# Loading the first experts' weights one round earlier on SyncE's queue, with two small edits beside it

## The chip, the cores and the metric

One Trainium2 chip, one of its cores. The metric is the time of one execution on the device, in microseconds. The kernel is one launch; nothing is computed on the host.

## The reference, cut to what matters

The inputs are x (32 sequences of 56 tokens, 256 wide, so 1792 tokens), a context of 32 x 1500 rows of 256, a mask, and the weights of four layers. Each layer normalizes x and adds its result to x:

```python
x = x + _L0_xattn_ref(_layernorm(x), ctx, ...)   # decayed running sum over 1500 context rows, two projections, mean, layernorm
x = x + _L0_ffn_ref(_layernorm(x), ...)          # 16 experts of 176, each token takes its best 6
x = x + _L1_xattn_ref(_layernorm(x), ctx, mask)  # attention over the masked context
x = x + _L1_ffn_ref(_layernorm(x), ...)          # 2 experts of 1024, each token takes 1
```

The layer that matters here is the second one:

```python
scores = softmax(h @ gate_w.T); topk_w, topk_idx = top_k(scores, 6)
for e in range(16):
    g = h @ w_gate[e].T; u = h @ w_up[e].T
    y = y + cw[:, e:e+1] * (silu(g) * u @ w_down[e].T)
```

## The kernel before, in words

**First stage, lines 228 to 904.** The context is read once, one sequence of 1.5 MB at a time, by SyncE's DMA queue (`load_ctx`, L155) into a ring of five slots. TensorE sums each sequence with the decay weights (`count_in`, L339); after it has used slot b it lets the load of sequence b + 5 begin. Two sequences share one tile of 128 rows, a pair; there are 16 pairs, 0 to 15. A loop of 15 rounds runs over a list written out by hand (`steps`, then `ends`, L751 to 765): each round handles several pairs at different depths. Round p counts the context of later pairs, projects and normalizes pair p, and for pair p - 1 writes the normalized rows: `second_norm` (ScalarE, L563) makes them in a tile of the pool `xn`, which has four buffers, so that the tile of pair p is that of pair p - 4; `away` (L569) stores it to the scratch tensor `xn0` in HBM over SyncE's queue. I call these norm p and store p. The same rows go on to the router: transposed (`turned`), gated (`gate`), the six best experts marked (`best`), ranked within their expert (`ranks`, `counted`, `places`), and sorted into blocks of 128 rows of one expert by products with one-hot matrices (`ones_at` on VectorE, `more_ones` on GpSimd, L674, `last_ones` on ScalarE, L692; `tokens_in`, ScalarE, L655, multiplies in the token numbers; `sorted_in`, TensorE, L702). Only two one-hot tiles exist, so those of pair p are written after the products of pair p - 1.

**After the loop** the last three pairs a, b, c = 13, 14, 15 are finished by a straight list of calls (L775 to 903), which ends with the table `idx` of the rows of each block (VectorE, L902) and the weights `wgt` (ScalarE, L903). `busy(n)` (L683) puts n products of 128 x 512 into TensorE's queue whose result nobody reads.

**The weights of the 16 experts** live in one tile, `w0_sb`. `load_w0_up` (L206) issues four transfers of 1408 KB for the gate and up halves, in rows of 704 bytes. `w0_down_pieces` (L222) yields 26 small transfers of 16 to 176 KB for the down half; `some_pieces(n)` issues the next n of them. All of this, like the context and the stores, is issued by SyncE in program order. In the built program every transfer of that queue uses one of eight completion counters in turn, and is issued only when the transfer eight places before it has landed.

**Second stage, L905 to 1230.** The experts run over 95 blocks. Block i needs its rows gathered from `xn0` by GpSimd's indirect DMA (L1092, the first eight together), transposed by TensorE (L191) and copied by ScalarE (L193), and then the gate and up products (L933), the transposes (L951) and the down products (L960). The weight of a block is addressed by a register, so the first gate-up product waits for every transfer into `w0_sb`, and the first gather for every store into `xn0`.

Of the kernel before, what the change touches and what calls it, by code (L numbers as in the profile page):

```python
# [22 lines left out]
NP = B // 2  # L23
# [37 lines left out]
def xattn_ffn_kernel(  # L61
# [141 lines left out]
    def load_w0_up():  # L203
        for m, w in ((0, wg0), (1, wu0)):
            for k in range(KD):
                nc.sync.dma_start(  # L206
                    out=w0_sb[:, :, (2 * k + m) * F0 : (2 * k + m + 1) * F0],
                    in_=w[:, k, :].rearrange("p (e f) -> p e f", f=F0),
                )

    def w0_down_pieces():

        half = E0 // 2
        for e in range(half):
            for c in range(2):
                r = 0
                while r < H0:
                    f = e * F0 + c * H0 + r
                    n = min(H0 - r, P - f % P)
                    o = 2 * KD * F0 + c * D  # L220
                    k = f // P
                    yield lambda r=r, n=n, e=e, o=o, f=f, k=k: nc.sync.dma_start(  # L222
                        out=w0_sb[r : r + n, e :: half, o : o + D],
                        in_=wd0[f % P : f % P + n, k :: half * F0 // P, :][:, 0:2, :],
                    )
                    r += n

    with tc.tile_pool(name="p1", bufs=1) as p1, tc.tile_pool(name="p3", bufs=3) as p3, tc.tile_pool(
# [185 lines left out]
        def first_stats(o):  # L414
            for p in range(o, o + 4):
                V.bn_stats(out=st[:, p, :], in_=xr[:, p, :])
                V.bn_aggr(out=mva[:, p, :], in_=st[:, p, :])
            inverse_root(rsa[:, o : o + 4], mva[:, o : o + 4, 1])

        def first_bias(o):  # L420
            q = slice(o, o + 4)
            V.scalar_tensor_tensor(nba[:, q], mva[:, q, 0], -1.0, rsa[:, q], ALU.mult, ALU.mult)
# [145 lines left out]
        def away(p):  # L568
            nc.sync.dma_start(out=xn0[p * P : (p + 1) * P, :], in_=pend[p]["xn"])  # L569
# [23 lines left out]
        def scores_out(p):  # L593
            A.copy(lgs[p % 2][:, 0:E0], pend[p]["lp"][:, 0:E0])
# [25 lines left out]
        def ranks(p):  # L620
            rk = ps.tile([P, 512], F32, tag="ps", name="rk")
            PE.matmul(rk[:, 0:E0], lhsT=before, rhs=sel[:, p, :], start=True, stop=False)
            PE.matmul(rk[:, 0:E0], lhsT=ones, rhs=chosen[:, 1 - p % 2], start=False, stop=True)
            keep(p, rk=rk)
# [7 lines left out]
        def places(p):  # L632

            nm, pr = pend[p]["nm"], pend[p]["pr"]
            V.tensor_scalar(lvl[:, p, :], pos[:, p, :], -0.5 - P / 2, ROUND, ALU.add, ALU.add)
            V.tensor_scalar(lvl[:, p, :], lvl[:, p, :], -ROUND, 1.0 / P, ALU.add, ALU.mult)
            off = small.tile([P, E0], F32, tag="off", name="off")
            V.scalar_tensor_tensor(
                off, lvl[:, p, :], -float(P), pos[:, p, :], ALU.mult, ALU.add
            )  # L640
            v = vals[:, p % 2]
            V.tensor_tensor(
                v[:, :, 0, :], e16.unsqueeze(1).to_broadcast([P, E0, NLP]),
                lvl[:, p, :].unsqueeze(2).to_broadcast([P, E0, NLP]), ALU.is_equal,
            )
            V.reciprocal(nm[:, 1:2], nm[:, 1:2])
            V.scalar_tensor_tensor(
                v[:, :, 1, :], v[:, :, 0, :], nm[:, 1:2],
                pr.unsqueeze(2).to_broadcast([P, E0, NLP]), ALU.mult, ALU.mult,
            )  # L650
            keep(p, off=off)

        def tokens_in(p):
            v = vals[:, p % 2]
            A.activation(v[:, :, 0, :], v[:, :, 0, :], AF.Copy, scale=ids[:, p : p + 1])  # L655

        def hots(p, h):
            t = pend[p].setdefault("hots", {})
            if h not in t:
                t[h] = ohp.tile([P, NE, P], F32, tag="oh", name="oh")  # L660
            return t[h]

        def ones_at(p, h, n=NE):

            o = NE * h
            V.tensor_tensor(
                hots(p, h)[:, 0:n], iota.unsqueeze(1).to_broadcast([P, n, P]),
                pend[p]["off"][:, o : o + n].unsqueeze(2).to_broadcast([P, n, P]), ALU.is_equal,
            )
# [9 lines left out]
        def busy(n, w=512):  # L679

            for _ in range(n):
                d = psa.tile([P, 512], F32, tag="acc", name="d")
                PE.matmul(  # L683
                    d[:, 0:w], lhsT=ident, rhs=ones[:, 0:1].to_broadcast([P, w]),
                    start=True, stop=True,
                )

        def last_ones(p, h, n):

            t, off = hots(p, h)[:, n:NE], pend[p]["off"]  # L690
            for i in range(n, NE):
                A.activation(  # L692
                    t[:, i - n], iota, AF.Abs, bias=off[:, NE * h + i : NE * h + i + 1], scale=-1.0
                )
            A.activation(t, t, AF.Relu, bias=ones[:, 0:1], scale=-1.0)
# [19 lines left out]
        def low_ones(p):  # L715
            ones_at(p, 0)
# [16 lines left out]
        pieces = list(w0_down_pieces())  # L733


        def some_pieces(n):
            for _ in range(n):
                if pieces:
                    pieces.pop(0)()
# [22 lines left out]
        for p in range(last):  # L762
            for step, d in steps if p == last - 1 else steps + ends:
                if 0 <= p + d < NP:
                    step(p + d)
            if p < 3:
                first_stats(4 * p + 4)
                first_bias(4 * p + 4)
            if p == NP - 4:
                load_w0_up()  # L770
            if p > NP - 4:
                some_pieces(6)


        at_ = slots[B % NRING].rearrange("p j d -> p (j d)")[0:1, CW - 2 * E0 * NLP :]  # L775
        G.memset(at_, 0.0)
        at_ = at_.rearrange("p (e o l) -> p e o l", e=E0, o=2)
        a, b, c = last - 2, last - 1, last
        scores_out(a)
        sum_in_columns(c)  # L780
# [24 lines left out]
        away(b)  # L805
        second_norm(c)
        away(c)
        some_pieces(len(pieces))
        places(a)
        turned(b)  # L810
        more_high_ones(a)
# [22 lines left out]
        PE.matmul(tot[:, 0:E0], lhsT=ones, rhs=chosen[:, b % 2], start=False, stop=True)  # L834
        more_high_ones(b)
        ranks(c)
        busy(2)
        real = p2.tile([P, NL, E0], F32, name="real")
        V.tensor_tensor(
            real, tot[:, 0:E0].unsqueeze(1).to_broadcast([P, NL, E0]), lev, ALU.is_gt  # L840
# [20 lines left out]
        for k in range(4):  # L861
# [3 lines left out]
                rhs=ones[0:1, 0:1], start=True, stop=True,  # L865
            )
        low_ones(c)
        last_ones(c, 1, 6)
        tokens_in(c)
        ones_at(c, 1, 6)  # L870
        sorted_low(c)
        blk = p2.tile([P, 4], F32, name="blk")
# [963 lines left out]
```

## Time and profile before

| | |
|---|---|
| runs before, us | 703.46 median of 3 (700.73 to 703.96) |
| profiled execution, us | 743.97, its span 742.3 |
| busy share of the span | PE 91%, PEld 59%, DVE 52%, POOL 43%, ACT 35% |
| mean granted TensorE clock | 0.955 |
| SyncE's queue (q1) | 56042 packets, 100.31 MB, 38.6% of 16 engines' span |
| first gather issued, us from the span's start | 180.53 |
| first gate-up product of the experts | 186.37 |

The profiled execution is 40.5 us longer than the median of the runs shown. PE is the matrix engine, PEld its weight loads, DVE VectorE, ACT ScalarE, POOL GpSimd; SPq is SyncE's queue, whose rows are DMA issues. A timeline row is: start in us, length in us, engine, line, operation, output<-input, count, and in brackets how long the engine was idle before it and what ended that. A row of a table by stretches has the busy us of each engine (count of instructions in parentheses), then the granted clock, then the DMA engines' busy share and their GB/s.

### The profile page before, as it was taken

The page shows a single profiled execution, that of the slowest core. Times are in us where ns is not written, and L with a number is a line of the kernel's source. Part 1 is how long each engine was busy: PE and PEld are TensorE (multiplying, and loading weights), DVE is VectorE, ACT ScalarE, POOL GpSimd, SP SyncE. Part 2 cuts the span into 40 slices and gives each one's busy share as a digit, 9 for nine tenths or more (in the row PEclk, how much of TensorE's full clock was granted, in tenths as well). Part 3 has the DMA queues.
Part 4 walks back from the last instruction along what each step waited for, and adds up shares of the span by engine and source line. Part 5 has one row for each costly group of instructions (what it writes and reads, how often), then busy time and mean ns, then how long its engine had stood idle before and what let it go on. Part 6 is the DMA issues. An engine that isn't in the chain of part 4 may idle for free.

```text
span 742.3 us, 13524 instructions
## 1 busy us (share of the span) xinstructions
PE 674.1 (91%) x4111; PEld 434.3 (59%) x4111; DVE 386.9 (52%) x1310; ACT 258.5 (35%) x772; POOL 318.0 (43%) x416
## 2 busy tenths in 40 slices
PE   7789999998799888898898888999897999999997
PEld 3345565654577565566676655566554666666564
DVE  5548888885256344343353436568787332323232
ACT  0224555542244333333343332476552111111110
POOL 3104454544543664667656655558423302122111
PEclk7858999998899999999999999999999999999999
DMA  8999999995489874444444444595941201010100
GB/s 272 337 406 404 410 411 411 384 287 147 133 260 282 292 217 149 121 128 128 135 128 136 128 124 119 149 329 79 333 143 62 88 15 33 32 38 28 35 30 18
DMA packets 71273, 136.63 MB, mean 184 GB/s; under 512 B 8026, under 2 KB 43772, under 8 KB 71196
## 3 DMA queue, kind: packets, MB, share of 16 engines
q1 hardware_dynamic: 56042, 100.31, 38.6%
q0 software_dynamic: 14096, 34.52, 17.1%
q10 hardware_dynamic: 1058, 0.86, 0.4%
q8 instruction: 38, 0.62, 0.4%
q14 instruction: 39, 0.32, 0.1%
HBM read 109.54 MB, written 26.77 MB: 184 GB/s over the span
## 4 chain that ended last, share of the span: by engine, by line
PE 65%; DVE 4%; issue 2%; ACT 2%; SPq 1%; DMA 1%; POOL 0%; another core or an unknown queue 0%; POOLq 0%; ACTq 0%; DVEq 0%
PE gu L933 30%; PE y L960 19%; PE tp L951 4%; PE tp L191 3%; PE tp L1064 3%; PE sp L1294 2%; PE op L1329 2%; SPq L222 1%; ACT xT L193 1%; PE tp L1053 1%; PE tp L1321 1%; PE sp L1288 1%; DMA w_sb<-in_wd 1%; DMA xs<-pay,to 0%; POOL oh L674 0%
## 5 line engine op out<-in xcount | busy, mean ns | idle before, releaser
L933 PE MATMUL gu<-w_sb,xT 128*128 x380 | 134.3, 476 | 29.4 <-ACT xT L193 19.8
L939 ACT ACTIVATE sg<-gu 128x176 f32<-128x176 f32 (+1 forms) x155 | 53.3, 344 | 247.0 <-PE gu L933 213.0
L1092 POOL DMA_INDIRECT xb<-xn,idx x95 | 94.0, 989 | 95.5 <-PE tp L191 43.3
L945 DVE SCALAR_TENSOR_TENSOR hs<-sg,wgt,gu 128x176 f32<-128x176 f32 x95 | 37.7, 397 | 154.5 <-ACT sg L939 129.2
L933 PE MATMUL gu<-ring,xT 128*128 x240 | 113.8, 597 | 0.0
L933 PEld LDWEIGHTS gu<-w_sb,xT 128*128 128x128 f32 x380 | 69.9, 192 | 65.4 <-ACT xT L193 27.8
L960 PE MATMUL y<-w_sb,hT 88*128 x380 | 98.6, 382 | 1.6 <-ACT yb L1100 1.6
L1007 POOL DMA_INDIRECT g<-ys,early x78 | 74.6, 956 | 35.3 <-issue 20.4
L943 DVE TENSOR_TENSOR hs<-sg,gu 128x256 f32<-128x256 f32 x60 | 25.3, 421 | 112.2 <-ACT sg L939 108.3
L951 PEld LDWEIGHTS tp<-ident,hs 128*88 128x88 f32 (+1 forms) x310 | 40.3, 130 | 58.7 <-issue 47.9
L960 PEld LDWEIGHTS y<-w_sb,hT 88*128 88x128 f32 x380 | 65.0, 191 | 7.4 <-ACT yb L1100 2.0
L1580 POOL DMA_INDIRECT out<-ob,ti x15 | 14.8, 990 | 126.9 <-DVE ob L1577 126.6
L674 POOL TENSOR_SCALAR oh<-iota,off 128x128 f32<-128x128 f32 x60 | 42.5, 722 | 59.0 <-PE owned L702 39.8
L953 DVE COPY hT<-tp 88x256 f32<-88x256 f32 (+1 forms) x155 | 64.4, 415 | 4.8 <-PE y L960 4.0
L933 PEld LDWEIGHTS gu<-ring,xT 128*128 128x128 f32 x240 | 45.6, 192 | 33.3 <-issue 30.5
L339 PE MATMUL acc<-ring,cz 128*32 128x256 f32 x768 | 57.0, 438 | 5.8 <-DMA ring<-in_cx 5.4
L960 PE MATMUL y<-ring,hT 128*128 x240 | 61.7, 380 | 0.0
L951 PE MATMUL tp<-ident,hs 128*88 128x128 f32 (+1 forms) x310 | 59.5, 274 | 0.0
L193 ACT COPY xT<-tp 128x256 f32<-128x256 f32 x110 | 41.0, 373 | 41.9 <-PE y L960 21.3
L1100 ACT COPY yb<-y 128x256 f32<-128x256 f32 x95 | 35.7, 376 | 47.0 <-PE y L960 27.2
L191 PE MATMUL tp<-ident,xb 128*128 128x128 f32 x220 | 42.5, 275 | 0.9 <-DMA xb<-xn,idx 0.9
L960 PEld LDWEIGHTS y<-ring,hT 128*128 128x128 f32 x240 | 41.0, 190 | 3.3
(315 smaller groups left out, 967.5 us busy)
## 6 DMA issues: line engine op xcount, KB each, us to landing
ring<-in_cx SPq DMA_DIRECT2D x32, 1536.0 KB
ys<-yb SPq DMA_DIRECT2D x95, 128.0 KB
ring<-in_cx SPq DMA_DIRECT2D x16, 384.0 KB
extra<-in_cx SPq DMA_DIRECT2D x16, 384.0 KB
xs<-zrow SPq DMA_DIRECT2D x5, 771.0 KB
w_sb<-in_wg SPq DMA_DIRECT2D x2, 1408.0 KB
w_sb<-in_wu SPq DMA_DIRECT2D x2, 1408.0 KB
xn<-xn SPq DMA_DIRECT2D x16, 128.0 KB
```

The lines of the kernel that those rows point to most:

```text
L191: PE.transpose(tp[:, k * P : (k + 1) * P], xn[:, k * P : (k + 1) * P], ident)
L193: A.copy(xT.rearrange("p k c -> p (k c)"), tp[:, 0 : KD * P])
L339: PE.matmul(acc[Q * g : Q * g + Q, 0:D], lhsT=cz[:, j, 1 - h : 1 - h + Q], rhs=c[:, j, :], start=(h == 0 and m == 0), stop=(h == 1 and m = ...
L674: G.tensor_scalar(hots(p, h)[:, i, :], iota, pend[p]["off"][:, NE * h + i : NE * h + i + 1], None, ALU.is_equal,)
L933: PE.matmul(gu[:, 0 : 2 * fp], lhsT=xT[i][:, k, :], rhs=w[:, bass.ds(at[i] + (u * piece + k * 2 * fp), 2 * fp)], start=(k == 0), stop=(k = ...
L939: A.activation(sg, gu[:, 0:fp], AF.Silu)
L945: V.scalar_tensor_tensor(hs[i, u], sg, wgt[:, i : i + 1], up, ALU.mult, ALU.mult)
L951: PE.transpose(tp[0:h, c * P : (c + 1) * P], a[:, c * h : (c + 1) * h], ident)
L953: V.tensor_copy(hT[i, u], tp[0:h, 0 : 2 * P])
L960: PE.matmul(y[i][:, 0:D], lhsT=a[:, c * P : (c + 1) * P], rhs=w[0:h, bass.ds(at[i] + (u * piece + doff + c * D), D)], start=(u == 0 and c ...
L1007: G.indirect_dma_start(out=g, out_offset=None, in_=ys0[0 : n * P, :], in_offset=bass.IndirectOffsetOnAxis(ap=at[:, p, k : k + 1], axis=0),)
L1092: G.indirect_dma_start(out=xb, out_offset=None, in_=xn0, in_offset=bass.IndirectOffsetOnAxis(ap=idx[:, i : i + 1], axis=0),)
```

## The change

In the loop, `load_w0_up` is called at the end of round 11 and not 12, and the rounds after it issue eight down pieces each and not six. The pieces that are left after the loop are issued ahead of everything in the list that follows, and not after the stores of pairs 14 and 15. One of two unread products after `ranks(c)` goes. `tokens_in(c)` is called ahead of `last_ones(c, 1, 6)`.

```diff
@@ -766,15 +766,16 @@
-            if p == NP - 4:
+            if p == NP - 5:
                 load_w0_up()
-            if p > NP - 4:
-                some_pieces(6)
+            if p > NP - 5:
+                some_pieces(8)
 
 
         at_ = slots[B % NRING].rearrange("p j d -> p (j d)")[0:1, CW - 2 * E0 * NLP :]
         G.memset(at_, 0.0)
         at_ = at_.rearrange("p (e o l) -> p e o l", e=E0, o=2)
+        some_pieces(len(pieces))
         a, b, c = last - 2, last - 1, last
@@ -805,7 +806,6 @@
         away(b)
         second_norm(c)
         away(c)
-        some_pieces(len(pieces))
         places(a)
@@ -834,7 +834,7 @@
         ranks(c)
-        busy(2)
+        busy(1)
@@ -865,8 +865,8 @@
         low_ones(c)
+        tokens_in(c)
         last_ones(c, 1, 6)
-        tokens_in(c)
         ones_at(c, 1, 6)
```

On SyncE's queue the order from the last context load on was: store 11, four gate/up loads, store 12, 6 pieces, store 13, 6 pieces, stores 14 and 15, 14 pieces. It becomes: four gate/up loads, store 11, 8 pieces, store 12, 8 pieces, store 13, 10 pieces, stores 14 and 15. No other engine's order changes but for the missing product on PE and the place of one instruction on ACT.

## The prediction

> **What bounds the kernel now.** I read the page first: TensorE is busy for 91% of the span, but the change touches only the passage from the router to the experts, so what counts is which wait ends last there. The chain of waits, in that stretch, says:
>
> ```profile
> 181.69 4.13 DMA w_sb<-in_wd
> 185.82 0.55 issue
> 186.37 1.56 PE gu L933 x4
> ```
>
> The last down piece is issued at 181.69, lands at 185.82, and lets the first gate-up product go at 186.37. After that the experts keep TensorE in work to the end, so a shift of this product shifts the end. Second, SyncE's own timeline, the queue whose order changes:
>
> ```profile
> 131.70 0.37 SPq L155 DMA_DIRECT2D ring<-in_cx  x1
> 134.89 0.34 SPq L569 DMA_DIRECT2D xn<-xn  x1
> 135.32 10.62 SPq L206 DMA_DIRECT2D w_sb<-in_wg  x2
> 146.00 9.35 SPq L206 DMA_DIRECT2D w_sb<-in_wu  x2
> 155.44 3.66 SPq L569 DMA_DIRECT2D xn<-xn  x1
> 159.14 4.88 SPq L222 DMA_DIRECT2D w_sb<-in_wd  x6
> 164.44 0.37 SPq L569 DMA_DIRECT2D xn<-xn  x1
> 165.06 4.82 SPq L222 DMA_DIRECT2D w_sb<-in_wd  x6
> 169.98 1.77 SPq L569 DMA_DIRECT2D xn<-xn  x2
> 171.80 10.74 SPq L222 DMA_DIRECT2D w_sb<-in_wd  x14
> ```
>
> From 135.32 on this queue hardly rests: the weights are as late as they are because it is never free. Two regimes must be told apart, by the table of stretches (its last three columns are granted clock, DMA share, GB/s):
>
> ```profile
> 134.00:136.00 2.00, 2.00 (x30) 0.92 (x26) 1.90 (x10) 1.14 (x4) 0.00 (x0) 1.00 1.03 410
> ...
> 158.00:160.00 2.00, 2.00 (x6) 0.93 (x5) 1.39 (x5) 0.50 (x2) 0.00 (x0) 1.00 1.15 334
> ...
> 168.00:170.00 2.00, 2.00 (x3) 0.96 (x4) 2.00 (x3) 0.67 (x4) 2.00 (x2) 0.50 0.45 106
> ```
>
> To about 162 the DMA engines are full (share above 1): the long issues of L206 are a full queue pushing back. After that they are half idle and the issue itself is the pace, 0.8 us for each piece.
>
> Last, who else arrives at the experts, and the two places at which the change will be felt:
>
> ```profile
> 160.99 1.08 ACT L563 ACTIVATE xn<-xr,mv 128x256 f32<-128x256 f32 x2
> ...
> 179.31 0.26 DVE L902 CAST idx<-bl 128x95 int32<-128x95 f32 x1 [1.48 <-PE bl L898]
> ...
> 180.53 1.19 POOL L1092 DMA_INDIRECT xb<-xn,idx  x1 [9.82 <-ACT wgt L903]
> ```
>
> The gathered rows are transposed, and ScalarE's copy of block 0 (L193) runs from 184.57 for 0.37: ready at 184.94, only 1.4 us before the product. So two chains end nearly together: weights (186.37) and rows (about 185.0).
>
> **Edit 1a, the four loads ahead of store 11.** Program order lets SyncE issue them after the context load at 131.70, at 132.1 and not 135.32: 3.2 us earlier. The Trainium skill's DMA: Bandwidth & Descriptors (Rules for kernel authors) advises to issue a transfer early and wait late. By that rule all that follows on the queue moves up 3.2 us. By the row it cannot: at 134 to 136 the engines move 410 GB/s of context already queued ahead, and the loads drain behind it whenever they are issued. All they gain is that store 11 no longer stands ahead: 128 KB / 410 GB/s = 0.3 us. I take the row. SyncE is then free for the first piece at 159.14 - 0.3 = 158.8.
>
> **Edit 1b, store 11 behind the loads.** It now takes the place that store 12 had, issued by 159. Store 12 landed just before 165.06: the piece issued then waited for it (SyncE's waits list 0.2 us at L222 for the store), since a transfer waits for the one eight places before it. So store 11 lands at 165.0 - 0.3 = 164.7. Norm 15 writes the buffer of norm 11, so it may not start before; the row of L563 shows it starting at 161.5. ScalarE stalls for 3.2 us, and behind it stand both row copies for the router (L581), so the gates of pairs 14 and 15, and everything down to `idx`.
>
> **Edit 1c, the last two stores behind all pieces.** 26 pieces cost 4.88 + 4.82 + 10.74 = 20.4 us. Between them now stand stores 12 and 13, about 0.45 each, and some 0.3 us of waits for counters: 158.8 + 20.4 + 0.9 + 0.3 = 180.4. So the last piece is issued 2.1 us sooner (182.54 before), and weights would land near 183. But stores 14 and 15 begin only then. Before, they began at 169.98, and the trace's semaphore record has GpSimd's wait for the last one end at 173.13, 3.15 us on: now 180.4 + 3.15 = 183.6. The first gather waits for them. Before, it started at 180.53, 0.96 after `idx` (179.57), and 4.5 us later block 0 could have begun (185.03). Now: 183.6 + 0.96 + 4.5 = 189.1, against 186.37. That is +2.7.
>
> **Edits 2 and 3.** The unread products:
>
> ```profile
> 167.81 3.76 PE L683 MATMUL d<-ones,ident 128*128 128x512 f32 x4
> 171.50 1.94 PE L702 MATMUL owned<-oh,vals 128*32 128x128 f32 x32
> ```
>
> Two products took 3.76 us at half clock; without one, the sort of pair 14 starts 1.9 sooner, though its upper half waits for GpSimd's one-hots to 170.7, so 1.7 are left. With the token numbers ahead of the two compares, the last sort (L702 at 175.27) no longer waits 0.63 for them. Downstream VectorE gains only the 0.4 it waited for the products, and the products for `idx` come after its last compare: 1.0 us in sum. Set against the stall: `idx` at 179.57 + 3.2 - 1.0 = 181.8, the gather could go at 182.7. The stores hold it until 184.6, so these edits are worth nothing while that cover stands, and 1.0 if it is gone. The skill's TensorE: Matmul & The Clock Gate (HAM oscillation) warns of idle gaps over 3.4 us; by it the missing product could cost the clock. In the row of 168 to 170 the clock is at 0.50 with both products there, so at this place nothing is left to lose. Bounds: 0 to -1.0.
>
> **The clock at the first blocks.** TensorE idles from 183 to 186 before block 0, and the chain shows block 0's gate-up at 1.56 and block 1's, from 188.82, at 2.48: the clock falls between. Now it idles till 189 (the unread products that fill the time end about 3.3 after `wgt`, near 185.4), so I expect block 0 to fall in the half clock as well: +0.9. Bounds: 0 (the drop moves with the work) and +2 (a third block too).
>
> **Sum:** 2.7 + 0.9 = 3.6 us, on 743.97 of the profiled execution 747.6. The 40.5 us between that and the median lie in places the page doesn't name; I carry the shift over unscaled: 703.46 + 3.6 = 707.1.
>
> **Rivals.** Forecast, 0.55: as above, 706.0 to 708.5.
> *Faster, 0.12:* in an execution without a profile the engines have room at 132, and the loads do begin 3.2 us early. Everything on SyncE moves up by that: store 11 lands at 161.5, norm 15 does not wait, the last stores land at 180.4, near `idx` (178.6). Then block 0 goes at about 185 to 184.0, 1.4 to 2.3 sooner: 701.6. It decides from a start of about 2.7 us earlier. Against it stands the DMA share of 1.03 and 410 GB/s.
> *About no change, 0.18:* half of that; store 11 and the last stores land 2 us sooner than I say: +0.7, 704.2. For it: the profile itself may slow transfers of 704-byte rows.
> *Worse, 0.15:* the 3.2 us that TensorE stands still at 162 take the clock away through the router's tail too. Products there run at half speed, about 2 us more, `idx` passes the stores, and two blocks start cold: +6, 709.5.
>
> **How the numbers follow.** 0.5%, 3.5 us, is about what a measurement of this kernel can tell from no change. Slower by more (over 707.0): 0.38 of the forecast's 0.55, and all of worse: 0.53. Within: 0.17 of the forecast, 0.18, and 0.08 of the faster case: 0.43. Faster: 0.04. The range leaves out most of the faster case and the end of the worse one: 703.5 to 710.
>
> **What would show it.** Right: SyncE's L206 issues end near 155 as before although they begin at 132; L563 shows an idle of about 3 us before norm 15; the last two L569 stand near 180; the first gather's idle is ended by a DMA xn<-xn, and block 0 starts near 189. Wrong: L206 done by 152, or a gather that starts within 1 us of `idx`.

## The result, and the profile after

| | before | changed |
|---|---|---|
| runs, us | 703.36 median of 7 (700.73 to 703.96) | 707.46 median of 7 (705.92 to 710.84) |
| ratio | | 1.0078 [1.0055, 1.01] |
| profiled execution, us (its span) | 743.97 (742.3); a second one 700.99 (699.2) | 707.22 (705.5) |
| first gather issued | 180.53; 180.97 | 185.73 |
| block 0's gate-up product | 186.37; 186.10 | 189.74 |
| block 1's gate-up product | 188.82; 188.24 | 191.87 |

The change costs 4.1 us by the medians (5.5 by the ratio, 3.9 to 7.0 by its interval), where 3.6 was forecast; 707.1 was predicted. One of the 22 runs of the experiment e3 below took 1122 us, at a mean granted clock of 0.552, and is left out of its ratio. The kernel before was profiled a second time, because the first profiled execution is 43 us longer than the second and so cannot be set beside the one of after. Comparisons with the kernel before are with the second from here on. In it block 1 comes 3.6 us sooner than in the changed kernel. The last context product (`count_in`, L339) starts at slightly different times in each trace, at 147.54 in the second profile before and at 147.04 in the changed kernel; measured from there, as in the table of runs below, the shift at block 1 is 4.1 us.

I had expected block 0 of the second profile to wait for the last down piece, as it does in the first. It does not; the rows come last in it:

```profile
186.10 1.45 PE L933 MATMUL gu<-w_sb,xT 128*128 x4 [0.52 <-ACT xT L193]
```

So of the two chains that the prediction has ending nearly together, which one is last changes from one execution to the next.

First the chain of waits in the changed kernel, from the store behind the loads to block 1 (start, length, engine, what):

```profile
154.93 9.59 DMA xn<-xn
164.60 0.61 ACT xn L563
...
181.44 0.44 SPq L569
181.99 2.85 DMA xn<-xn
184.90 0.83 issue
185.73 3.00 DMA xb<-xn,idx
188.81 0.42 PE tp L191 x2
189.32 0.38 ACT xT L193
189.74 1.47 PE gu L933 x4
...
191.87 1.45 PE gu L933 x4
```

Where a down piece stood in the chain of the first profile, there are now two stores: store 11, which takes 9.59 us to land and lets ScalarE's norm 15 go at 164.60, and store 15, which lands at 184.84 and lets the first gather go. SyncE's timeline of the changed kernel:

```profile
130.39 15.32 SPq L206 DMA_DIRECT2D w_sb<-in_wg  x2
145.76 9.06 SPq L206 DMA_DIRECT2D w_sb<-in_wu  x2
154.93 3.72 SPq L569 DMA_DIRECT2D xn<-xn  x1
158.69 7.10 SPq L222 DMA_DIRECT2D w_sb<-in_wd  x8
165.90 0.46 SPq L569 DMA_DIRECT2D xn<-xn  x1
166.41 6.26 SPq L222 DMA_DIRECT2D w_sb<-in_wd  x8
172.78 0.45 SPq L569 DMA_DIRECT2D xn<-xn  x1
173.27 8.07 SPq L222 DMA_DIRECT2D w_sb<-in_wd  x10
181.44 0.91 SPq L569 DMA_DIRECT2D xn<-xn  x2
```

and the same rows of the kernel before, second profile:

```profile
134.16 12.11 SPq L206 DMA_DIRECT2D w_sb<-in_wg  x2
146.32 9.04 SPq L206 DMA_DIRECT2D w_sb<-in_wu  x2
155.46 3.66 SPq L569 DMA_DIRECT2D xn<-xn  x1
159.16 4.88 SPq L222 DMA_DIRECT2D w_sb<-in_wd  x6
```

The loads begin 3.8 us sooner and their issue ends 0.5 sooner (154.82 against 155.36). Since the whole changed trace is 0.5 us ahead at the last context product, nothing is left of that when both are measured from there: the issue ends 7.8 us after it in either kernel. Third, the engines of the changed kernel at the two places named in the prediction, norm 15 and `idx` with the gather:

```profile
164.60 0.60 ACT L563 ACTIVATE xn<-xr,mv 128x256 f32<-128x256 f32 x1 [5.74 <-DMA xn<-xn]
...
184.00 0.26 DVE L902 CAST idx<-bl 128x95 int32<-128x95 f32 x1 [1.48 <-PE bl L898]
...
185.73 1.19 POOL L1092 DMA_INDIRECT xb<-xn,idx  x1 [10.90 <-DMA xn<-xn]
```

ScalarE stands still for 5.74 us; `idx` is done at 184.26, and 0.6 us later the last store is down. Two delays thus arrive at the gather almost together. Last, the stretches around the stall and the start of the experts (granted clock, DMA share and GB/s at the end):

```profile
134.00:136.00 2.00, 2.00 (x26) 1.29 (x30) 1.66 (x7) 0.80 (x3) 2.00 (x3) 1.00 1.01 410
...
158.00:160.00 2.00, 0.44 (x2) 0.20 (x2) 1.49 (x8) 0.83 (x3) 0.76 (x2) 1.00 1.16 314
160.00:162.00 2.00, 0.00 (x0) 0.00 (x0) 0.60 (x1) 0.00 (x0) 2.00 (x3) 0.75 1.04 291
162.00:164.00 2.00, 0.00 (x0) 0.00 (x0) 0.00 (x0) 0.00 (x0) 0.14 (x1) 0.50 0.74 192
...
168.00:170.00 2.00, 2.00 (x19) 1.93 (x23) 1.33 (x6) 0.68 (x4) 1.00 (x1) 0.50 0.47 110
...
188.00:190.00 2.00, 0.67 (x3) 0.46 (x4) 0.00 (x0) 0.67 (x2) 1.39 (x3) 1.00 0.29 92
```

At 134 the DMA engines move as many bytes as before (410 GB/s, as in the prediction's row). TensorE does nothing from 160 to 164, while store 11 is on its way through DMA engines that are full to 162 and still busy for 0.74 of the time after it.

### The profile page after: what moved, and what is told of

It reads as the page before. It is cut to its first block, busy times and chain, and to the rows that moved or that the text cites. A ratio compares the mean times of both kernels' runs of the same rounds, so it can differ in the third digit from the quotient of the medians.

```text
span 705.5 us, 13520 instructions
## 1 busy us (share of the span) xinstructions
PE 660.4 (94%) x4109; PEld 435.7 (62%) x4109; DVE 386.8 (55%) x1310; ACT 261.2 (37%) x772; POOL 314.9 (45%) x416
## 4 chain that ended last, share of the span: by engine, by line
PE 73%; DMA 13%; DVE 6%; SPq 2%; ACT 2%; issue 1%; POOL 1%; POOLq 0%; DVEq 0%; ACTq 0%
PE gu L933 30%; PE y L960 19%; DMA ring<-in_cx 7%; PE tp L951 5%; PE acc L339 4%; DMA xn<-xn 4%; PE tp L191 3%; DMA xs<-pay,to 2%; PE tp L1064 2%; PE sp L1294 1%; PE sT L520 1%; PE op L1329 1%; SPq L222 1%; SPq L250 1%; PE bp L531 1%
## 5 line engine op out<-in xcount | busy, mean ns | idle before, releaser
L933 PE MATMUL gu<-w_sb,xT 128*128 x380 | 129.7, 463 | 2.8 <-ACT xT L193 1.4
L1092 POOL DMA_INDIRECT xb<-xn,idx x95 | 91.7, 965 | 66.3 <-PE tp L191 37.5
L339 PE MATMUL acc<-ring,cz 128*32 128x256 f32 x768 | 56.3, 433 | 8.1 <-DMA ring<-in_cx 7.7
L193 ACT COPY xT<-tp 128x256 f32<-128x256 f32 x110 | 40.9, 372 | 22.7 <-PE tp L191 21.8
```

The lines of the kernel that those rows point to most:

```text
L193: A.copy(xT.rearrange("p k c -> p (k c)"), tp[:, 0 : KD * P])
L339: PE.matmul(acc[Q * g : Q * g + Q, 0:D], lhsT=cz[:, j, 1 - h : 1 - h + Q], rhs=c[:, j, :], start=(h == 0 and m == 0), stop=(h == 1 and m = ...
L933: PE.matmul(gu[:, 0 : 2 * fp], lhsT=xT[i][:, k, :], rhs=w[:, bass.ds(at[i] + (u * piece + k * 2 * fp), 2 * fp)], start=(k == 0), stop=(k = ...
L1092: G.indirect_dma_start(out=xb, out_offset=None, in_=xn0, in_offset=bass.IndirectOffsetOnAxis(ap=idx[:, i : i + 1], axis=0),)
```

## The experiments

Three theories stood after this. A: the stall of norm 15 alone makes the loss (`idx` is late). B: the stores behind all pieces alone make it (the gather is held). C: both, as two chains beside each other that end nearly together, so that the loss is that of the later one and not the sum, and mending one leaves the other.

**e1, the two small edits alone.** Store and load order as before.

```diff
-        busy(2)
+        busy(1)
...
-        last_ones(c, 1, 6)
         tokens_in(c)
+        last_ones(c, 1, 6)
```

> Edits 2 and 3 alone: one unread product less and the token numbers ahead of the two compares, SyncE's order as before. My theory (the weights end last in the kernel before, and these edits only speed up the rows' chain): no change, within 0.7 us of before, ratio 0.999 to 1.001. Rival (the missing product costs the half clock in the router's tail or at the first blocks): 1 to 2 us slower, ratio 1.002 to 1.003.

Measured: 1.0001 [0.9982, 1.002]. They are worth nothing. From the last context product, `idx` starts 0.3 us sooner than before (31.88 against 32.22), and block 0 not at all (38.61 against 38.56). The row of block 0 in this kernel says why:

```profile
184.95 1.42 PE L933 MATMUL gu<-w_sb,xT 128*128 x4 [1.85 <-DMA w_sb<-in_wd]
```

It waits 1.85 us for the last down piece. In this execution the weights are the later of the two chains, and what the rows gain is lost in front of them. e1 is what the next two are compared with, since they contain these edits.

**e3, the loads early, the last stores where they were.** e1, and:

```diff
-            if p == NP - 4:
+            if p == NP - 5:
                 load_w0_up()
```

> Edits 2 and 3, and of edit 1 only the four gate and up loads one round sooner, ahead of store 11; the stores of pairs 14 and 15 keep their place before the last 14 pieces. My theory (store 11 lands at 164.6 behind the loads and holds up the norm of pair 15, ScalarE stands still for 5 us, and the router's tail runs at half clock): idx still ends near 184.2, the first gather follows at once near 185.2, ratio 1.005 to 1.008, so nearly all of the loss although the late stores are gone. Rival (the late stores are the cause, as my sum had it): idx waits, but the loss is under 1 us, ratio 0.999 to 1.002.

Measured: 1.0042 [1.0027, 1.0057], medians 705.8 against 702.92: less than I expected, and more than the rival allows. Its rows of norm 15, `idx` and the first gather:

```profile
164.13 0.60 ACT L563 ACTIVATE xn<-xr,mv 128x256 f32<-128x256 f32 x1 [5.91 <-DMA xn<-xn]
...
183.56 0.26 DVE L902 CAST idx<-bl 128x95 int32<-128x95 f32 x1 [1.48 <-PE bl L898]
...
184.77 1.19 POOL L1092 DMA_INDIRECT xb<-xn,idx  x1 [10.41 <-DMA w_sb<-in_wd]
```

The stall is there, the stores are not in the way (they are issued at 170.15), and the gather starts 0.95 us after `idx` is done, as it does where nothing else holds it. The releaser printed beside the gather is a transfer that happened to end in that time. Counted from the last context product, `idx` is 5.3 us later than in e1, block 0 3.7: the 1.5 us between them are hidden behind the 1.85 us that block 0 of e1 waits for weights in any case.

**e6, the last stores behind all pieces, the loads where they were.** e1, and the rest of the pieces issued ahead of the list after the loop:

```diff
         at_ = at_.rearrange("p (e o l) -> p e o l", e=E0, o=2)
+        some_pieces(len(pieces))
...
         away(c)
-        some_pieces(len(pieces))
```

> Edits 2 and 3, and of edit 1 only the order at the end: all down pieces ahead of the stores of pairs 14 and 15; the gate and up loads stay behind store 11. My theory (two chains of nearly equal length, of which either alone is enough): norm 15 doesn't wait, idx ends near 178 to 180, but the first gather waits for the last store until about 185, ratio 1.005 to 1.008. Rival (the stall of ScalarE alone makes the loss): ratio 0.998 to 1.002.

Measured: 1.0061 [1.004, 1.0082], medians 707.22 against 702.92. Its rows of norms 14 and 15, `idx`, the gather and block 0:

```profile
159.66 1.08 ACT L563 ACTIVATE xn<-xr,mv 128x256 f32<-128x256 f32 x2
...
177.97 0.26 DVE L902 CAST idx<-bl 128x95 int32<-128x95 f32 x1 [1.48 <-PE bl L898]
...
185.22 1.19 POOL L1092 DMA_INDIRECT xb<-xn,idx  x1 [15.85 <-DMA xn<-xn]
...
189.45 2.71 PE L933 MATMUL gu<-w_sb,xT 128*128 x4 [0.52 <-ACT xT L193]
```

No stall, and `idx` is done at 178.23, but the gather goes only at 185.22: it is held by the stores for 6 us more than the 0.95 that it needs. And block 0 takes 2.71 us and not 1.45. So either half of edit 1 alone slows the kernel, and neither A nor B alone is enough.

**e4, the changed kernel without the stall.** A fifth buffer in the pool `xn` lets norm 15 go without store 11:

```diff
-        name="xn", bufs=4
+        name="xn", bufs=5
```

> The changed kernel with five tiles for normalized rows. My theory (the late stores alone are enough): idx ends near 178, the gather still waits until about 184.8 for the last store, ratio 1.005 to 1.008, no better than the changed kernel. Rival (the stall of ScalarE made the loss): ratio 0.998 to 1.002.

Measured: 1.0077 [1.0049, 1.0105], no better than the changed kernel at 1.0078. Norm 15 does not wait; `idx` is done at 180.53, 2.5 us later than I expected but still 5.2 before the gather:

```profile
185.71 1.19 POOL L1092 DMA_INDIRECT xb<-xn,idx  x1 [16.06 <-DMA xn<-xn]
```

The stall was made to go, and nothing was won, because the stores end at the same time as ever. This is what C says and A doesn't; e3, which loses without late stores, is what C says and B doesn't.

**e5, the loads early, no stall, no late stores.** e3 with the same fifth buffer.

> As the run with only the loads early, but the pool of normalized rows has five tiles and not four, so that norm 15 writes the tile of pair 10, whose store stands ahead of the loads. My theory (the loss of 2.9 us comes from norm 15's wait for store 11): ScalarE's idle of 5.9 us before norm 15 is gone, idx ends near 178.5, the weights end last again, ratio 0.997 to 1.002. Rival (the early loads cost by something else, such as the context loads being slowed): the loss stays, ratio 1.003 to 1.006.

Measured: 0.999 [0.9972, 1.0008]. The loss of e3 is gone whole, so it was the stall. The run says one thing more: the loads are issued as early as in the changed kernel here, with nothing in their way, and they bring nothing that can be told from zero. In its profile block 0 starts 0.95 us sooner than in e1 (37.66 against 38.61 after the last context product), but it takes 2.23 us where e1's takes 1.42, and block 1 is level (40.78 against 40.71):

```profile
185.37 2.23 PE L933 MATMUL gu<-w_sb,xT 128*128 x4 [1.76 <-DMA w_sb<-in_wd]
```

Whether the early loads or the chance of one execution moved block 0, one profile does not tell.

**e7 and e8, stores 12 to 15 taken off SyncE's queue.** e7 is e1, and e8 the changed kernel with five buffers, each with

```diff
-            nc.sync.dma_start(out=xn0[...], in_=pend[p]["xn"])
+            (nc.scalar if p > NP - 5 else nc.sync).dma_start(out=xn0[...], in_=pend[p]["xn"])
```

> Edits 2 and 3, SyncE's order as before, but the stores of pairs 12 to 15 are issued by ScalarE on its own queue, so that SyncE issues only weights after store 11. My theory: four stores of 0.4 to 0.5 us and their waits leave SyncE's queue, the last piece is issued about 2 us sooner, weights land near 182.9, block 0 starts when its rows are ready, near 183.7, 1.3 to 2.4 us sooner than before: ratio 0.9965 to 0.9985. Rival (issuing on ScalarE delays the router's tail by as much as it saves, 4 issues of about 0.4 us): ratio 0.999 to 1.002.

> The changed kernel with both of its waits taken away by other means: five tiles for normalized rows, and the stores of pairs 12 to 15 issued by ScalarE on its own queue. My theory: neither norm 15 nor the first gather waits for a store behind the weights; weights land near 183, idx ends near 178.3, block 0 starts near 183.7: ratio 0.9965 to 0.9985, and the whole difference to the changed kernel, 5 to 7 us, is those two waits. Rival (early loads cost something of their own): ratio above 1.001.

Measured: e7 0.9998 [0.9981, 1.0015], e8 0.9992 [0.9976, 1.0008]. With both delays mended the changed kernel's loss is gone whole (1.0078 to 0.9992), which completes C. The gain that I expected beyond that, down to 0.9965 to 0.9985 in both, did not come. In e8 SyncE issues the 26 pieces in one go,

```profile
159.41 23.35 SPq L222 DMA_DIRECT2D w_sb<-in_wd  x26
```

but in 23.35 us where the three issues of the changed kernel make 21.43, and the list of SyncE's waits (total, times, longest) holds

```profile
SPq L222 <- DMA xn<-xn: 3.0, 1, 3.0
```

In e7 the same row says 4.7, and the 26 pieces take 27.36. In the built program both queues draw on the same eight completion counters, so a piece still waited for a store that had been issued at about 160 into full DMA engines, though it stood on another engine's queue. So the weights ended where they did before, and block 0 of e8 waits for them:

```profile
186.11 1.42 PE L933 MATMUL gu<-w_sb,xT 128*128 x4 [1.88 <-DMA w_sb<-in_wd]
```

The runs that carry the argument, by start in us after the last context product:

| | order of loads and stores | `idx` | first gather | block 0 | block 1 | ratio |
|---|---|---|---|---|---|---|
| before, second profile | old | 32.22 | 33.43 | 38.56 | 40.69 | |
| e1 | old | 31.88 | 33.09 | 38.61 | 40.71 | 1.0001 |
| e3 | loads early | 37.15 | 38.36 | 42.35 | 44.49 | 1.0042 |
| e5 | loads early, 5 buffers | 30.13 | 31.34 | 37.66 | 40.78 | 0.999 |
| e6 | stores last | 30.23 | 37.48 | 41.71 | 45.31 | 1.0061 |
| changed | both | 36.96 | 38.68 | 42.70 | 44.83 | 1.0078 |
| e4 | both, 5 buffers | 31.92 | 37.36 | 41.57 | 45.17 | 1.0077 |
| e7 | old, other queue | 32.66 | 33.87 | 38.41 | 41.06 | 0.9998 |
| e8 | both, 5 buffers, other queue | 31.78 | 32.99 | 38.71 | 40.81 | 0.9992 |

Against e1 the gather goes 5.3 us later for the stall alone (e3), 4.4 for the stores alone (e6), and 5.6 for both (changed): near the larger of the two and far from their sum. At block 1 these are 3.8, 4.6 and 4.1; e6 pays the clock there (below). That the loss is not the sum rests on the traces: the ratios alone, 0.42, 0.61 and 0.78% with intervals of 0.15 to 0.23 to either side, are too coarse for it, and they put the changed kernel 2.5 us behind e3, where the traces have 0.3 at block 1.

Differences in `idx` of 2 us and less are not to be read: in the kernels without a stall it starts anywhere from 30.13 to 32.66. The granted clock of TensorE differs on the way there; from 162 to 170 it was 1.00 in e5 and 0.50 in e1. No version was found that is faster than the kernel before beyond the interval.

## Why the prediction was right, and where its sizes were off

**1a, loads begun early gain only 0.3 us: right.** Measured from the last context product they begin 3.3 us sooner, their issue ends at the same time, and the last of them lands 17.2 us after that product where it was 17.3; in e5 nothing comes of it that the timed runs can tell. That everything would move up by 3.2 us was my reading of the page. The row of the Trainium skill's DMA: Bandwidth & Descriptors (Rules for kernel authors) says only that the fixed setup cost of a transfer issued early overlaps with compute, not that the transfer lands earlier. Into engines that were moving 410 GB/s, these loads did not.

The faster rival (701.6) and the one of about no change (704.2) are out by the timed runs of the changed kernel, 705.92 to 710.84, and by the landings of store 11 (164.52) and store 15 (184.84), neither of which came 2 us sooner than I said. A gain of up to 2 us by early loads alone is not excluded: e5's interval reaches down to 0.9972.

**1b, norm 15 waits for store 11: right, the size too small.** The store lands at 164.52 (164.7 in the prediction), but the wait is 5.74 us and not 3.2. The landing was well placed, the time at which ScalarE wanted to go was not. I took it from the row of L563 in the first profile, 160.99. In the second profile of the same kernel:

```profile
158.77 1.08 ACT L563 ACTIVATE xn<-xr,mv 128x256 f32<-128x256 f32 x2
```

That is 2.2 us sooner, while SyncE's queue in the two profiles agrees to 0.1 us at 155. In the execution that I worked from, the engines ran late and the DMA didn't, and a stall is the difference of the two. So `idx`, forecast for 181.8, was done at 184.26. No other size was so far off. It does not show in the sum, because the stores held the gather in any case: without them the gather could have gone at about 185.2, and it went at 185.73. The forecast had a cover of 1.9 us there (182.7 against 184.6); the longer wait left 0.5.

**1c, the last stores behind the pieces: right, 1.2 us late.** 26 pieces took 21.43 and not 20.4 us: store 15 landed at 184.84 against 183.6, the gather started at 185.73 against 184.6, block 0 at 189.74 against 189.1. The place of block 0 is off by less than its parts, as the gather to block 0 took 4.0 us where I had 4.5.

**Edits 2 and 3, nothing while the cover stands, 1.0 us if it is gone: the first not tested, the second not found.** No run takes them out of the changed kernel, where the stores hold the gather. In e1, where no late store covers them, they bring nothing (1.0001). The missing product did give back its time, as the changed kernel's row has it, 2.05 us for one where the two took 3.76:

```profile
172.97 2.05 PE L683 MATMUL d<-ones,ident 128*128 128x512 f32 x2
```

In e1 there is another cover that I had not counted: the weights hold block 0 for 1.85 us. Of the 1.0 us forecast for `idx` e1 shows 0.3; one execution of each does not tell more.

**The clock at the first blocks, +0.9: wrong in this kernel.** The fall that I built on (1.56 us, then 2.48) is in the first profile alone, where TensorE did not rest from 183 to 186 throughout but for 0.89 and 1.89 us with two transposes between; in the second, blocks 0 and 1 take 1.45 us each. In the changed kernel they take 1.45 us each as well, in the stretch of 188 to 190 at a granted 1.00. The unread products after `wgt` (L909) fill TensorE's idle time:

```profile
184.58 3.29 PE L909 MATMUL d<-ones,ident 128*128 128x512 f32 x8 [0.62 <-ACT wgt L903]
188.81 0.41 PE L191 MATMUL tp<-ident,xb 128*128 128x128 f32 x2 [0.95 <-DMA xb<-xn,idx]
```

I had them end near 185.4, 3.7 us ahead of block 0. The longer stall moved them to the end of the wait, where only 0.95 us is left idle. In e6 and e4, where `idx` is early, the idle time is what I had in mind, and the price with it. e6:

```profile
178.55 3.29 PE L909 MATMUL d<-ones,ident 128*128 128x512 f32 x8 [0.62 <-ACT wgt L903]
188.27 0.66 PE L191 MATMUL tp<-ident,xb 128*128 128x128 f32 x2 [6.44 <-DMA xb<-xn,idx]
```

Block 0 then takes 2.71 us, 1.26 more, and in e4, after an idle time of 4.60, 2.72. The length of one gap does not settle it, though: in e5, after 1.48 and 1.76 us idle with two transposes between, block 0 took 2.23 us, and in e1, after 0.60 and 1.85, 1.42. So in the changed kernel the stall gave back in the clock what it took at the gather. This is also why mending it alone (e4) brought nothing: e4's gather goes 1.3 us sooner than the changed kernel's (37.36 against 38.68), but at block 1 it is 0.3 behind.

**The worse rival** had one half of its mechanism come true: TensorE stood still at 162 and the granted clock was 0.50 from 162 to 180. But the tail of the kernel before is at 0.50 for most of its length as well:

```profile
162.00:166.00 4.00, 3.96 (x42) 3.50 (x43) 3.26 (x14) 1.00 (x5) 2.91 (x5) 0.50 0.69 186
166.00:170.00 4.00, 4.00 (x9) 2.03 (x9) 3.69 (x10) 1.05 (x5) 2.74 (x3) 0.50 0.45 128
```

So there was little left to lose: from the start of norm 15 to `idx` the changed kernel takes 19.4 us and the kernel before 20.5. And the changed kernel's blocks 0 and 1 did not start cold.

**The sum.** 2.7 for the gather and 0.9 for the clock made 3.6. Measured by the traces' own times it is 3.6 at block 1, all of it the gather's, none the clock's; measured from the last context product 4.1. That this is also the difference of the medians is in part chance, as the next lines show. The total was right by luck in one respect: a term that was too small and one that was too large made up for each other.

What stays open: in the one profile of the changed kernel another 1.7 us are lost between blocks 30 and 40. From the last context product, block 30 runs 4.1 us later than before, and blocks 40 to 94 5.8; in e6 block 50 runs 4.6 later. The granted clock falls there in the changed kernel,

```profile
282.00:286.00 4.00, 3.05 (x9) 1.81 (x10) 0.01 (x1) 1.16 (x3) 1.36 (x2) 0.74 0.39 123
286.00:290.00 4.00, 4.00 (x19) 3.17 (x18) 1.88 (x8) 1.43 (x4) 2.18 (x3) 0.84 0.29 79
```

and in e6, at the same block, it does not:

```profile
282.00:286.00 4.00, 2.70 (x13) 1.54 (x12) 1.08 (x6) 1.63 (x5) 2.22 (x3) 1.00 0.50 151
```

TensorE was idle for 0.96 and 0.43 us just before the fall, but so it was at this block in the kernel before, where the clock stayed at 1.00. e4, e6 and the changed kernel have the same time within their intervals, so I take it for the difference of one execution; no run tells.

## What to carry to other kernels

Issued 3.3 us earlier into DMA engines that were full, at 410 GB/s, the loads here were no further on at the end; the new order only chose what landed behind them. So ask of each small transfer that a load overtakes who waits for it: here ScalarE for a buffer, and GpSimd for the last rows. When two things are late at one gate, mending one of them may show nothing, as in e4 (1.0077 against 1.0078); mend each alone and both together before dropping a cause. A wait worked out as the difference of two rows needs both from an execution that stands for the others, and a profile that is 40 us from the median asks for a second one before its small differences are used.

## What the runs showed that was not expected

Two profiled executions of the same kernel differed by 43 us (742.3 and 699.2), and up to the start of the experts what moved was the compute against the DMA: norm 14 by 2.2 us, SyncE's store at 155 by 0.02. The bulk lies behind that: from block 0 to block 94 the first takes 38 us more. From 190 to 470 its gate-up products wait 19 times for ScalarE's copy of the rows (L193), 19.8 us in all, and those of the second once, for 0.5. Why the copies came late I did not find out.

A transfer put on ScalarE's queue still held up SyncE's, by 3.0 us in e8 and 4.7 in e7, because the program's eight completion counters are shared by both queues. In e8 the fifth piece was held until 165.62; the store that had the same counter before it was issued by ScalarE at 159.25 and landed at 165.60.
